# Half of the cross-attention transposes moved from TensorE to VectorE blocks and a trip through DRAM

## The chip, the cores and the metric

The kernel runs on one core of a Trainium2 chip. The metric is the time of one execution on the device in microseconds (us), the median of three runs. All times below come from the runs and from one profiled execution of the kernel before the change.

## What is computed

One decoder layer in float32 on `x` of shape (8, 256, 1024) with a context of the same shape: self-attention, cross-attention and a gated feed-forward network, each after a layer norm and each added to its input. Only the middle part is changed. Cut to it, the reference is

```python
def _L0_xattn_ref(Q, K, Wq_d, W_qk, Wkv_d, Wv_u):       # Q = layernorm(x), K = context
    C_q = Q @ Wq_d                                       # 1024 -> 128
    C_kv = K @ Wkv_d                                     # 1024 -> 64
    CqWqk = (C_q @ W_qk).reshape(b, n, H, LKV)           # 16 heads of 64
    scores = jnp.einsum('bnhl,bkl->bhnk', CqWqk, C_kv) / jnp.sqrt(...)
    attn = jax.nn.softmax(scores, axis=-1)
    V_up = (C_kv @ Wv_u).reshape(b, nkv, H, HD)
    out = jnp.einsum('bhnk,bkhd->bnhd', attn, V_up)
```

For each of the 8 batches and 16 heads there is a 256x256 matrix of probabilities. It is computed with the queries on the partitions, and its product with the values needs it the other way round, with the keys on the partitions. So every such matrix is turned. How it is turned is what the change is about.

## The kernel before, in words

**Stages.** The program runs self-attention for the 8 batches (64 steps of four heads), then cross-attention for the 8 batches (32 steps of four heads), then the feed-forward network. The loop at L1657-L1668 makes the steps. A batch of cross-attention has four steps, called c0 to c3 here.

**One cross step** is `step()` at L733, for the heads `j` = 0 to 3 of `cur`; `prev` is the step before, `due` the one before that. In the order in which each engine gets its instructions:

- `scores` (L669): TensorE multiplies the queries with the latent keys, 8 matmuls into four PSUM banks `pss0` to `pss3`, one per head. Each bank has one buffer, so a head's scores wait until the exponentials of that head in the step before have read it.
- `due.early()` (L707): VectorE copies the weighted product `po` of the step before last to `ol`.
- Per head, VectorE takes the maximum of each row (L743), and `turned(prev.p[j])` (L575) turns the previous step's probabilities: TensorE makes four 128x128 transposes into PSUM (L579) and ScalarE copies the result to the tile `pT` (L583).
- `due.late()` (L711): four matmuls with the value weights (L716), VectorE scales with 1/sum (L724), GpSimd adds to the residual rows `x1t` (L731).
- The exponentials: 8 ScalarE instructions, two per head (L762), each with a row sum. They are mixed with the *parts* of the queue: `step` keeps an account in which a part has a planned cost in us and an exponential 0.49, and issues exponentials ahead of a part as long as they are behind it.
- `prev.weighted(pTs)` (L693, called at L798) at the end of the step: 8 matmuls (L699) of the turned probabilities with the latent values, into `po`.

**Parts** are pieces of work for the next batch, written out by hand in `cross_plan` (L1501): in c0 two of the four `cqk` products (L941, L944) and the context's turning (L185); in c1 `ckv` (L855); in c2 `cq` (L925, copied by VectorE at L930); in c3 the small transposes L877, the first two `cqk` products, and `lnx` `first` (L904). In the first three batches an output projection of self-attention (`o_parts`) lies in some steps too, and three steps of the last batch hold a product of 16 large matmuls for the feed-forward network (L1123).

**`lnx` `first`** serves the batch after next. `send` normalises the rows (`normed_half`, L155, four 128x512 VectorE instructions at L157) and SyncE stores them to DRAM `n2` (L894). `take` reads them back in another order (`quarters_load`, L165: 32 partitions per DMA, four DMAs per tile, 1 KB runs, L168), so that 32x32 block transposes on VectorE (`turn32`, L181) make a full transpose of them. The same trick serves the context.

**Queues.** Each engine takes its instructions in program order (`tc.manual_schedule`, L1593). All loads, and all stores but those of GpSimd, are issued by SyncE in that order too, and a DMA that has to wait holds up the ones behind it. The feed-forward weights are loaded in the middle of cross-attention: `ffn_load_a` (L966) in c0 of batch 3, `ffn_load_b` (L977) in c0 of batch 4. `Head.norm` (L1073) normalises rows for the feed-forward network on GpSimd in c1 and c2 of batch 5 and in c3 of batch 6, each with a store by SyncE (L1080).

Of the kernel before, what the change touches and what calls it, by code (L numbers as in the profile page):

```python
# [18 lines left out]
P = 128  # L19
# [16 lines left out]
def decoder_layer(  # L36
# [117 lines left out]

    def normed_half(x_, mv, rs, h, tag="xn"):  # L155
        xn = wk_.tile([P, 512], F32, tag=tag, name="xn", bufs=2)
        nc.vector.tensor_scalar(  # L157
            xn, x_[:, h * 512 : (h + 1) * 512], mv, rs, ALU.subtract, ALU.mult
        )
        return xn  # L160
# [413 lines left out]

    def turned(p):  # L575
        ps = bank([P, TB, S], "ps_pt")
        for k in range(TB):
            for t in range(TB):
                nc.tensor.transpose(  # L579
                    ps[:, k, t * P : (t + 1) * P], p[:, t, k * P : (k + 1) * P], ident  # L580
                )
        pT = wk_.tile([P, TB, S], F32, tag="pT", name="pT", bufs=4)
        nc.scalar.copy(pT, ps)  # L583
        return pT

    class Self:


        def __init__(self, st, c):
            self.st, self.c = st, c  # L590

            self.by = st.by[c]
# [70 lines left out]
    class Cross:  # L663


        def __init__(self, st, c):
            self.st, self.c = st, c

# [24 lines left out]
        def weighted(self, pTs):  # L693

            self.po = pso.tile([P, 2, S], F32, tag="pso", name="po")
            for i in range(2):
                for k in range(TB):
                    for j in range(2):
                        nc.tensor.matmul(  # L699
                            self.po[XD * j : XD * (j + 1), i, :],  # L700
                            self.st.ckvT[:, k, :],
                            pTs[2 * i + j][:, k, :],
                            start=(k == 0),
                            stop=(k == TB - 1),
                        )

        def early(self):  # L707
            self.ol = wk_.tile([P, 2, S], F32, tag=("oh0a", "oh0b")[self.c % 2], name="ol")
            nc.vector.tensor_copy(self.ol, self.po)

# [22 lines left out]
    def step(cur, prev, parts, extra=None):  # L733
# [3 lines left out]
        cur.sm = small.tile([P, TB, 4], F32, tag="sm", name="sm")  # L737
        due = prev.prev if prev is not None else None
        if due is not None:
            due.early()  # L740
        pTs = []
        for j in range(4):
            nc.vector.tensor_reduce(nm[:, j, :], s[j], AX.X, ALU.max, negate=True)  # L743
            if prev is not None:
                pTs.append(turned(prev.p[j]))
        for p in queue[: min(parts, 2)]:
# [12 lines left out]
        def exp(j, t):  # L759
            if t == 0:  # L760
# [3 lines left out]
                bias=nm[:, j, t : t + 1], accum_out=cur.sm[:, t, j : j + 1],  # L764
            )

        exps = [(j, t) for j in range(4) for t in range(TB)]
# [29 lines left out]
        if prev is not None:  # L797
            prev.weighted(pTs)  # L798
            prev.prev = None
# [117 lines left out]
    def cq_part(st):  # L917
        box = {}

        def main(half):  # L920
# [258 lines left out]
    def unit(db, k, following, mid=None, jobs=((),) * 4, also=((),) * 3, sums_=(), last=False):  # L1179
# [39 lines left out]
        act(q7, c21)  # L1219
        ac2 = wide("pT", "ac2", 4)  # L1220
        stt(ac2, c12, bu, q7, ALU.add, ALU.add)  # L1221
# [279 lines left out]
    def cross_plan(b):  # L1501
# [91 lines left out]
    with tc.manual_schedule(  # L1593
# [257 lines left out]
```

## Time and profile before

| | |
|---|---|
| median of the 3 runs | 1460.16 us (1460.09 to 1461.78) |
| time of the profiled execution | 1462.0 us |
| its span, first to last instruction | 1460.2 us |
| granted TensorE clock, mean | 0.993 |
| busy share of the span: TensorE, VectorE, ScalarE, GpSimd | 97%, 74%, 58%, 42% |
| cross-attention, first to last scores | 629.1 to 949.1 us |
| one batch of it (799.97 to 837.54) | 37.57 us: steps of 9.25, 8.86, 10.22 and 9.24 |

The profile shows one execution. A group line names the source line, the engine, the operation, what is written and read, the count, the busy time and the mean duration in ns; behind the bar stands the idle time of the engine before these instructions and what ended it. In the trace, PE stands for TensorE's matmuls, PEld for its weight loads, DVE for VectorE, ACT for ScalarE, POOL for GpSimd and SP for SyncE. A float32 matmul other than a transpose is recorded as two instructions. Busy records overlap where matmuls are pipelined, so the duration of a group on the chain of waits tells its cost better than the mean duration of one.

### The profile page before, as it was taken

The page shows a single profiled execution, that of the slowest core. Times are in us where ns is not written, and L with a number is a line of the kernel's source. Part 1 is how long each engine was busy: PE and PEld are TensorE (multiplying, and loading weights), DVE is VectorE, ACT ScalarE, POOL GpSimd, SP SyncE. Part 2 cuts the span into 40 slices and gives each one's busy share as a digit, 9 for nine tenths or more (in the row PEclk, how much of TensorE's full clock was granted, in tenths as well). Part 3 has the DMA queues.
Part 4 walks back from the last instruction along what each step waited for, and adds up shares of the span by engine and source line. Part 5 has one row for each costly group of instructions (what it writes and reads, how often), then busy time and mean ns, then how long its engine had stood idle before and what let it go on. Part 6 is the DMA issues. An engine that isn't in the chain of part 4 may idle for free.

```text
span 1460.2 us, 25787 instructions
## 1 busy us (share of the span) xinstructions
PE 1422.7 (97%) x8946; PEld 954.7 (65%) x8946; DVE 1073.5 (74%) x2042; ACT 849.6 (58%) x2553; POOL 610.5 (42%) x769
## 2 busy tenths in 40 slices
PE   6899999999999999989999999999999999999998
PEld 6778888888888888667787777654444444444444
DVE  6888898989898989866777778447747645555664
ACT  4777898989898988856556666543313322223320
POOL 2544444444444443402232262435525424555740
PEclk9999999999999999989999999999999999999999
DMA  9620010101010124344448676723222000213003
GB/s 213 135 59 16 30 59 30 59 30 59 31 62 27 45 63 163 105 103 130 134 128 271 199 249 175 230 89 131 84 61 72 29 0 34 82 58 129 1 0 116
DMA packets 102961, 134.75 MB, mean 92 GB/s; under 512 B 44538, under 2 KB 75440, under 8 KB 102704
## 3 DMA queue, kind: packets, MB, share of 16 engines
q1 hardware_dynamic: 98224, 116.33, 27.2%
q0 software_dynamic: 4608, 16.78, 3.0%
q8 instruction: 72, 1.18, 0.3%
q14 instruction: 57, 0.47, 0.1%
HBM read 90.60 MB, written 41.94 MB: 91 GB/s over the span
## 4 chain that ended last, share of the span: by engine, by line
PE 54%; ACT 2%; DVE 2%; DMA 1%; issue 1%; SPq 0%; POOL 0%; ACTq 0%; DVEq 0%
PE c L1189 17%; PE z L1283 9%; PE ps_pt L579 4%; PE ps_o L1399 4%; PE s L676 4%; PE ps_p L1123 4%; PE po L699 3%; PE ps_o L716 2%; PE ps_q L925 2%; PE ps_qk L941 2%; ACT p L762 2%; PE ps_k L855 1%; PE ps_o L547 1%; PE ps_h L1252 0%; DMA n<-xn 0%
## 5 line engine op out<-in xcount | busy, mean ns | idle before, releaser
L762 ACT ACTIVATE p<-s,nm 128x256 f32<-128x256 f32 x768 | 358.4, 518 | 3.3 <-DVE nm L743 3.3
L583 ACT COPY pT<-ps_pt 128x512 f32<-128x512 f32 x384 | 197.7, 600 | 146.1 <-PE ps_pt L579 146.1
L743 DVE TENSOR_REDUCE nm<-s 128x2 f32<-128x512 f32 x384 | 237.5, 679 | 5.0 <-PE s L676 3.7
L579 PE MATMUL ps_pt<-ident,p 128*128 128x128 f32 x1536 | 198.9, 282 | 5.8 <-DVE p L623 2.5
L579 PEld LDWEIGHTS ps_pt<-ident,p 128*128 128x128 f32 x1536 | 167.4, 143 | 46.2 <-issue 24.2
L762 ACT ACTIVATION_READ_ACCUMULATOR p<-s,nm 128x1 f32 x768 | 191.8, 250 | 0.0
L1240 POOL TENSOR_TENSOR ac<-ac,sg 128x512 f32<-128x512 f32 x41 | 52.2, 1273 | 207.5 <-ACT sg L1239 207.5
L731 POOL TENSOR_TENSOR x1t<-x1t,y 128x256 f32<-128x256 f32 x64 | 46.3, 743 | 200.5 <-DVE y L724 200.5
L407 POOL TENSOR_SCALAR tmp<-y 128x512 f32<-128x512 f32 x78 | 60.1, 770 | 167.4 <-DVE y L556 91.3
L1189 PE MATMUL c<-t,s_v 128*128 128x512 f32 x252 | 122.2, 594 | 1.1 <-ACT q L1213 0.8
L454 PE MATMUL ps_q<-xh,qT_w 128*128 128x256 f32 x496 | 122.4, 288 | 0.0
L454 PE MATMUL ps_q<-xl,qT_w 128*128 128x256 f32 x496 | 119.6, 282 | 0.0
L1199 ACT COPY a<-c 128x512 f32<-128x512 f32 x42 | 24.6, 585 | 153.6 <-PE c L1189 153.6
L547 PE MATMUL ps_o<-oT_w,oh 128*128 128x512 f32 x256 | 106.4, 416 | 0.0
L547 PE MATMUL ps_o<-oT_w,ol 128*128 128x512 f32 x256 | 101.7, 397 | 0.0
L454 PEld LDWEIGHTS ps_q<-xh,qT_w 128*128 128x128 f32 x496 | 93.5, 188 | 1.6
L454 PEld LDWEIGHTS ps_q<-xl,qT_w 128*128 128x128 f32 x496 | 93.7, 189 | 0.0
L623 DVE TENSOR_SCALAR p<-p,sm 128x256 f32<-128x256 f32 x256 | 86.7, 396 | 8.4 <-PE ps_q L454 0.5
L1189 PEld LDWEIGHTS c<-t,s_v 128*128 128x128 f32 x252 | 47.4, 190 | 62.6 <-issue 50.3
L630 ACT ACTIVATE p<-p,sm 128x256 f32<-128x256 f32 x172 | 75.8, 513 | 18.9 <-DVE sm L613 18.3
L1221 DVE SCALAR_TENSOR_TENSOR ac<-c,b_col,q 128x512 f32<-128x512 f32 x42 | 31.5, 751 | 65.9 <-ACT q L1219 65.9
L600 PE MATMUL s<-kT,qT 32*128 32x256 f32 x1024 | 76.4, 403 | 3.7 <-DVE qT L412 2.4
(194 smaller groups left out, 3081.5 us busy)
## 6 DMA issues: line engine op xcount, KB each, us to landing
xs<-in_x_dram SPq DMA_DIRECT2D x32, 512.0 KB
x<-xs POOLq DMA_DIRECT2D x16, 512.0 KB, 3.1
x1t<-x SPq DMA_DIRECT2D x16, 512.0 KB
c<-in_ctx_dram SPq DMA_DIRECT2D x64, 128.0 KB
n<-xn SPq DMA_DIRECT2D x32, 256.0 KB
xp<-n SPq DMA_DIRECT2D x64, 128.0 KB
x<-x1t POOLq DMA_DIRECT2D x16, 512.0 KB, 5.6
x2n<-x SPq DMA_DIRECT2D x16, 512.0 KB
```

What stands on the lines that cost most here:

```text
L407: nc.gpsimd.tensor_scalar(tmp, y, 0.0, -1e6, ALU.min, ALU.max)
L454: nc.tensor.matmul(ps[:, i, :], w(i, e), x_[:, e, :], start=(e == 0 and x_ is st.xh), stop=(e == EC - 1 and x_ is st.xl),)
L547: nc.tensor.matmul(ps, o_[c // 4][:, c % 4, t * P : (t + 1) * P], oT_w[:, c, h * 512 : (h + 1) * 512], start=(c == 0 and o_ is st.oh), sto ...
L579: nc.tensor.transpose(ps[:, k, t * P : (t + 1) * P], p[:, t, k * P : (k + 1) * P], ident)
L583: nc.scalar.copy(pT, ps)
L600: nc.tensor.matmul(s[j][:, t, :], st.qT[p0 : p0 + 32, c, t * P : (t + 1) * P], st.kT[p0 : p0 + 32, c // 4, :], start=True, stop=True,)
L623: nc.vector.tensor_scalar_mul(p, p, self.sm[:, t, j : j + 1])
L630: nc.scalar.activation(p, p, AF.Copy, scale=self.sm[:, t, j : j + 1])
L743: nc.vector.tensor_reduce(nm[:, j, :], s[j], AX.X, ALU.max, negate=True)
L762: nc.scalar.activation(cur.p[j][:, t, :], s[j][:, t, :], AF.Exp, bias=nm[:, j, t : t + 1], accum_out=cur.sm[:, t, j : j + 1],)
L1189: nc.tensor.matmul(ps, w, x_, start=start, stop=stop, skip_group_check=True)
L1283: nc.tensor.matmul(db.X[key], w, x_, start=start, stop=stop or key == "1")
```

## The change

In each cross step, heads 2 and 3 are turned as before. Heads 0 and 1 go another way. As soon as their exponentials are done in their own step, VectorE turns them in 32x32 blocks into a tile `pB`, SyncE stores `pB` to DRAM (512 KB), and four DMAs (128 KB each, 1 KB runs, 32 partitions each) read it back with the quarters exchanged. The result `pD` holds the keys on the partitions, with the queries in runs of 32, and the weighted product reads it through a strided view. Since this takes time, the weighted product of a cross step is issued one step later: after the scores of the step after next, ahead of the transposes, with heads 2 and 3 first.

Other edits make room for it. The copy of `po` to `ol` goes from VectorE to ScalarE. The copy of `cq` goes from VectorE to ScalarE, and so does every other copy of `cqk` for the batches 1 to 7. The normalisation in `lnx` goes from VectorE to GpSimd. Tiles change places: `pT` has two buffers of two heads instead of four of one, `ol` uses the `v` buffers, `cq` a buffer of its own.

```diff
-    def normed_half(x_, mv, rs, h, tag="xn"):
+    def normed_half(x_, mv, rs, h, tag="xn", eng=None):
         xn = wk_.tile([P, 512], F32, tag=tag, name="xn", bufs=2)
-        nc.vector.tensor_scalar(
+        (eng or nc.vector).tensor_scalar(
...
+    both = [None]
+
+    def turned(p, j):
...
+        if j % 2 == 0:
+            both[0] = wk_.tile([P, 2, TB, S], F32, tag="pT", name="pT", bufs=2)
+        pT = both[0][:, j % 2]
         nc.scalar.copy(pT, ps)
         return pT
 
+    moved = [
+        dram.tile([P, 4, 2, P], F32, name=f"moved{i}") for i in range(B * XH // 4)
+    ]
+    crossed = [0]
+
+    def turned_blocks(cur):
+        n = crossed[0]
+        crossed[0] += 1
+        pB = wk_.tile([P, 4, 2, 4, 32], F32, tag="oh0b", name="pB")
+        for j in range(2):
+            src = cur.p[j].rearrange("p t (k c e) -> p c (t k) e", k=TB, c=4)
+            nc.vector.transpose(pB[:, :, j], src)
+        shape = [P, 4, 2, TB, TB, 32]
+        if n % 2:
+            pD = wk_.tile(shape, F32, tag="oh0a", name="pD")
+        else:
+            pD = wk_.tile(shape, F32, tag="pT", name="pD", bufs=2)
+        nc.sync.dma_start(moved[n], pB.rearrange("p c j m q -> p c j (m q)"))
+        for c in range(4):
+            nc.sync.dma_start(
+                pD[32 * c : 32 * c + 32].rearrange("p a j t k q -> p a (j t k q)"),
+                moved[n].rearrange("(a r) c j m -> r c a (j m)", a=4)[:, c],
+            )
+        for j in range(2):
+            cur.blocks[j] = pD[:, :, j]
+
+    def keys_of(pT, k):
+        if len(pT.shape) == 3:
+            return pT[:, k, :]
+        return pT[:, :, :, k, :].rearrange("p a t q -> p t a q")
+
+    def turned_of(prev, j):
+        return prev.blocks[j] if j in prev.blocks else turned(prev.p[j], j)
...
         def weighted(self, pTs):
             self.po = pso.tile([P, 2, S], F32, tag="pso", name="po")
-            for i in range(2):
+            for i in (1, 0):
...
-                            pTs[2 * i + j][:, k, :],
+                            keys_of(pTs[2 * i + j], k),
...
         def early(self):
-            self.ol = wk_.tile([P, 2, S], F32, tag=("oh0a", "oh0b")[self.c % 2], name="ol")
-            nc.vector.tensor_copy(self.ol, self.po)
+            self.ol = wk_.tile([P, 2, S], F32, tag="v", name="ol", bufs=2)
+            nc.scalar.copy(self.ol, self.po)
...
         due = prev.prev if prev is not None else None
+        if isinstance(due, Cross):
+            due.weighted(due.pTs)
         if due is not None:
             due.early()
...
-                pTs.append(turned(prev.p[j]))
+                pTs.append(turned_of(prev, j))
...
+            if (j, t) == (1, TB - 1) and not divided:
+                turned_blocks(cur)
...
         if prev is not None:
-            prev.weighted(pTs)
+            if isinstance(prev, Self):
+                prev.weighted(pTs)
+            prev.pTs = pTs
             prev.prev = None
...
-                    ("xn", "z")[t] if st.b > 1 else "xn",
+                    ("xn", "z")[t] if st.b > 1 else "xn", nc.gpsimd,
...
-                st.cq = wk_.tile([P, S], F32, tag="v", name="cq", bufs=2)
-                nc.vector.tensor_scalar_mul(st.cq, ps, 1.0 / 8.0)
+                st.cq = wk_.tile([P, W], F32, tag="cq", name="cq")[:, 0:S]
+                nc.scalar.activation(st.cq, ps, AF.Copy, scale=1.0 / 8.0)
...
-        k, q, t, u = ckv_part(x_), cq_part(x_), ckvT_part(x_), cqk_parts(x_, (dve, act))
+        k, q, t, u = ckv_part(x_), cq_part(x_), ckvT_part(x_), cqk_parts(x_, (act, act))
...
+        prev.prev.weighted(prev.prev.pTs)
         prev.prev.early()
-        pTs = [turned(p) for p in prev.p]
+        pTs = [turned_of(prev, j) for j in range(4)]
```

In the feed-forward network the tile `ac2`, which shares the `pT` buffers, is taken in pairs as well, and its last one uses the `cq` buffer.

More of the change, by code (lines that the diff above doesn't have):

```diff
@@ L572, in o_parts @@
         return [Part(2.0, lambda i=i: main(i)) for i in range(2)]
-    def turned(p):
+    both = [None]
+    def turned(p, j):
         ps = bank([P, TB, S], "ps_pt")
@@ L581, in turned @@
                 )
-        pT = wk_.tile([P, TB, S], F32, tag="pT", name="pT", bufs=4)
+        if j % 2 == 0:
+            both[0] = wk_.tile([P, 2, TB, S], F32, tag="pT", name="pT", bufs=2)
+        pT = both[0][:, j % 2]
         nc.scalar.copy(pT, ps)
         return pT
+    moved = [
[28 more added lines that the diff above has]
+        return prev.blocks[j] if j in prev.blocks else turned(prev.p[j], j)
     class Self:
         def __init__(self, st, c):
-            self.st, self.c = st, c
+            self.st, self.c, self.blocks = st, c, {}
             self.by = st.by[c]
@@ L666, in __init__ @@
         def __init__(self, st, c):
-            self.st, self.c = st, c
+            self.st, self.c, self.blocks = st, c, {}
         def scores(self):
@@ L1219, in unit @@
         act(q7, c21)
-        ac2 = wide("pT", "ac2", 4)
+        if k == FULL - 1:
+            ac2 = wide("cq", "ac2", 1)
+        else:
+            if k % 2 == 0:
+                both[0] = wk_.tile([P, 2, W], F32, tag="pT", name="ac2", bufs=2)
+            ac2 = both[0][:, k % 2]
         stt(ac2, c12, bu, q7, ALU.add, ALU.add)
```

## The prediction

> **What bounds the kernel now.** The chain of waits by engine comes first.
>
> ```profile
> PE 54%; ACT 2%; DVE 2%; DMA 1%; issue 1%; SPq 0%; POOL 0%; ACTq 0%; DVEq 0%
> ```
>
> TensorE carries almost all of it. (The chain could be followed back to 591 us only; the change acts behind that.) Next is one batch of cross-attention, first by busy times in a window, then as the chain in the order of time.
>
> ```profile
> 799.97:837.54 37.57, 37.52 (x293) 29.13 (x293) 27.45 (x54) 23.99 (x82) 7.70 (x12) 1.00 0.66 195
> ```
>
> ```profile
> 805.19 2.86 ACT p L762 x12
> ...
> 808.09 1.13 PE s L676 x6
> 809.22 1.98 PE ps_pt L579 x16
> 811.20 0.99 PE ps_o L716 x8
> 812.18 1.90 PE ps_k L855 x32
> ...
> 814.27 1.88 PE po L699 x16
> 816.14 1.93 PE s L676 x16
> ```
>
> TensorE is busy for 37.52 of 37.57 us, so a step lasts as long as its matmuls. But ScalarE shows in the chain at 805.19: its exponentials ended just late enough to hold the scores. It is idle a third of the time, yet it is the next limit.
>
> **TensorE's gain.** The 16 transposes of a step take 1.98 us, 0.124 each. Eight go: 0.99 us a step, 31.7 us in 32 steps, if nothing else becomes late. The moved product costs the same 1.88. Its strided operand has no row: from 0 (the same L699 row) to double for the four matmuls on it, +0.94 a step or +30 in all. I take 0, the row being the same instruction, and keep the other end. A gain is excluded, since columns and passes stay.
>
> **ScalarE's chain.** Let E be the end of a step's scores. Before, the transposes follow at E, the first copy to `pT` starts at E+0.7 (828.98 after 828.30), the exponentials at E+2.6 (830.89). After, the product (1.88) comes first, and ScalarE has the copy of `ol` at the head of its queue, behind it. It starts at E+2.1 (0.25 from a matmul's end to a copy, as in the rows); it and two `pT` copies, 0.51 apart like the four in 2.05, end at E+3.65. The exponentials start 1.05 later than before. They come 0.45 apart; the last score bank is free 0.15 after the eighth; three more matmuls (0.72) end the next scores. Copies of parts stand between the exponentials, where the account of L775 puts them, and wait for their matmuls (`late` ends at E+3.84):
> - c1: 3.65 + 3.6 + 0.15 + 0.72 = 8.1 (before 8.86).
> - c2: six exponentials, then `cq` at 3.84 + 3.46 + 0.25 = 7.55, 0.35 long, two exponentials: 9.7 (before 10.22).
> - c3: one exponential, the first `cqk` copy at 5.4, two exponentials, the second copy to 7.3, five exponentials: 10.4 (before 9.24).
> - c0: a `cqk` copy at 5.05, two exponentials, another to 6.95, six exponentials: 10.5 (before 9.25).
>
> A batch takes 38.7 against 37.6: 0.99 less on TensorE, and 1.1 more by ScalarE. Over six batches that is +7; the seven steps with `o_parts` or feed-forward matmuls stay bound by TensorE and gain 0.5 to 1 each, -5. **Sum of the loop: about +3.**
>
> **VectorE** gets two transposes (0.67 each, L185) and loses the `ol` copy (0.64): +0.7 a step, 2.8 a batch. It loses two `cqk` copies, a `cq` copy and four normalisations: 1.4 + 0.4 + 1.9. It is less busy than before (27.45 of 37.57), so I cost it at nothing; its cover would be gone if a transpose waited for `pB`, whose store must have landed.
>
> **The trip through DRAM.** The blocks of step n are needed in step n+2, in the second half of the product. Their DMAs stand in SyncE's queue behind whatever the step issued before. In that queue a wait holds up all the rest:
>
> ```profile
> SPq L894 <- DVE xn L157: 65.8, 10, 17.9
> SPq L1080 <- POOL x2n L1077: 43.6, 8, 18.8
> ...
> SPq L168 <- DMA w_ffn<-in_L_ffn_V_dram: 7.9, 1, 7.9
> ```
>
> The normalisation moves to GpSimd. The same operation on twice the width stands there already:
>
> ```profile
> L1077 POOL TENSOR_SCALAR x2n<-x2n,mv,rs x8: 3767/3771/3793, 853.2 to 921.3; 128x1024 f32<-128x1024 f32 x8
> ```
>
> Half of 3771 is 1.89 us, so four take 7.5 where VectorE's L157 took 1.9. The lowest row for the width is L407 (immediate operands, 0.77), the highest 3.77; I take 1.89 as it is the same operation. In c3 the account issues three exponentials ahead of `lnx`, and head 1's second, which releases the blocks, behind it. So the four `n2` stores and eight `xp` loads go ahead of the blocks. From E of c3: GpSimd's residual adds end at 6.3, the normalisations at 13.9, the last store lands at 16.5 (2.0 for a store, in the chain), the loads are issued by 18.5, their data (1 MB at 229 GB/s, window 838 to 842) flow until 20.5. The blocks' store (512 KB at 348 GB/s, window 842.5 to 845.5, 1.5, and 1.3 of latency, what is left of a 256 KB store's 2.01) lands at 22.8, their loads (2.3 of data, 1.3, 0.4 of issue) at 26.6. Needed at 10.4 + 10.5 + 0.94 = 21.9. **TensorE waits 4.3 to 4.7 us**, and as the `ol` copy and all exponentials stand behind it on ScalarE, nothing catches up. Six batches: **+26**.
>
> **Feed-forward loads.** In batch 3 c0 they are issued behind those late blocks (the fourth load at 22.8 + 1.8 = 24.6, which is 14.2 from c0's own E, 10.4 later), and c0's own blocks come behind them: 1 MB at 229 and 3.26 MB at 421 GB/s (window 776 to 782) with 1.3 of latency give E+27.6, the small bias loads 2, store 2.8, loads 4.0: E+36.4. Needed at 10.5 + 12.7 (c1 with its wait) + 0.94 = 24.1: **+12**. Five smaller ones: 2 MB of loads in c0 of batches 4 and 5 (6 us each at 348 GB/s against about 3.5 of slack), stores behind L1077 in batches 5 and 6 (7.5 and 15 us), eight loads more in c3 of batch 5: about 2.6 each, **+13**.
>
> **The clock.** TensorE's waits bring a second cost. Three windows show it, with the granted clock third from the right:
>
> ```profile
> 593.72:597.13 3.41, 1.06 (x6) 0.69 (x7) 3.37 (x7) 2.74 (x7) 1.95 (x2) 1.00 0.70 242
> 597.13:600.55 3.42, 3.42 (x11) 2.79 (x10) 2.64 (x7) 3.38 (x13) 1.68 (x3) 0.50 1.05 279
> ...
> 631.27:634.68 3.41, 0.95 (x8) 0.72 (x7) 1.50 (x5) 0.32 (x1) 0.00 (x0) 1.00 0.50 186
> 634.68:638.09 3.41, 2.69 (x10) 1.69 (x10) 3.41 (x8) 3.18 (x9) 0.00 (x0) 0.50 0.92 281
> ```
>
> A window that TensorE filled by 1.06 or 0.95 of 3.41 us was followed by one at half the clock, in the second case by three. One such window costs up to 1.7 us of work. Eight waits of 3 us and more (six, batch 3, batch 7): **+14**.
>
> The Trainium skill, "TensorE: Matmul & The Clock Gate", Part 1, has the gate close after a whole idle window of about 3.4 us. These rows are stricter: a third of a window busy did not prevent it. By the rule, our waits of 4.3 would seldom hold a whole window, and these 14 us would be near 0; I go by the rows. The skill's "VectorE: DVE Perf Modes", section "The three transpose paths", speaks against the change: VectorE turns 32x32 blocks only, and a whole 128x128 transpose belongs to TensorE. Its figures (311 ns against 390 in bf16) would make it a fair exchange; the trace's, 0.67 for a head against 0.50 plus a copy, say so too. What the rule leaves out is the trip for the rest.
>
> **Start of the stage.** Between 592 and 597 and between 631 and 635 VectorE waited for `xn` buffers while normalising, and TensorE stood for 2.4 and 2.6 us. With GpSimd these go (-3 to -8, with the clock), but the first batch's rows arrive some 6 us later, and VectorE waits for them. I take 0.
>
> **Sum**: 3 + 26 + 12 + 13 + 14 = +68 on the profiled execution's 1462.0 (span 1460.2), **1530 us**. The median of the runs is 1.8 lower, far inside the range.
>
> **Rivals.**
> - *The blocks come in time* (0.20). GpSimd normalises in 0.77 like L407, which saves 4.5 a batch and thereby the 26, and the loads hide. What is left is the loop with its +3 and some of the 25 at the feed-forward loads: 1463 to 1485. For it: VectorE and SyncE have room. Against: the L1077 row.
> - *TensorE's gain comes through* (0.12), the case on the other side: 1462 - 32 = 1430. It decides if exponentials end before TensorE's 7.7 us of a step. ScalarE would have to lose 1.1 a batch, 0.3 a step, for a gain to appear at all, and 2.8 in c0 for the whole. Against: its copies wait for a product and for `cqk` in program order.
> - *The clock stays low* (0.10), as for 10.2 us from 634.68 on: 8 waits cost up to 5 each, and doubled strided reads would add as much: 1570 to 1610.
> - That the change does not do what it says can't be: 256 transposes leave TensorE by the diff.
>
> **The numbers.** Forecast 0.58, rivals 0.20, 0.12, 0.10. The range leaves out the gain (0.12) and the worst of the slow rival (0.08): 1462 to 1595. A measurement tells 0.2% (3 us) from no change: faster 0.12, same 0.05 (a quarter of the first rival), slower 0.83.
>
> **What would show it.** Right: L579 has 1280 transposes; TensorE's longest waits are at L699 for a DMA of `pD`, in c1 of each batch and most in c2 of batch 3; L157 on GpSimd is near 1.9 us; windows at clock 0.5 in the middle of the stage; ScalarE's chain in c3 and c0. Wrong: no DMA in TensorE's waits; L157 below 1 us; c0 below 9.3 us.

## The result, and the profile after

The changed kernel takes 1567.9 us (median of four runs, 1566.2 to 1571.1); on the same chip the kernel before takes 1461.0. The ratio is 1.073, with an interval of 1.071 to 1.075: **107 us slower**. The forecast was 1530, slower with a chance of 0.83. The profiled execution took 1568.5, with a span of 1566.4 and a mean granted clock of 0.959 (before 0.993). Its lines are numbered by the changed file: the scores stand at L715, the product at L738, the transposes at L581, the exponentials at L803, the blocks at L602 (VectorE), L608 (store) and L610 (loads).

The chain of waits by engine, on the page of the changed kernel:

```profile
PE 42%; DMA 6%; POOL 6%; SPq 3%; DVE 2%; issue 2%; ACT 2%; DVEq 0%; POOLq 0%; ACTq 0%
```

DMA has grown from 1% to 6% and POOL from 0 to 6%, and SyncE's queue stands there with 3%. One batch, from the end of c0's scores in batch 4 to the same point of batch 5, as a window (length, then busy time of TensorE, its weight loads, VectorE, ScalarE and GpSimd, granted clock, DMA share, GB/s):

```profile
843.81:897.33 53.52, 41.14 (x262) 29.01 (x263) 27.19 (x52) 23.89 (x81) 17.50 (x17) 0.88 0.73 219
```

The same batch took 37.57 us, with TensorE busy for 37.52 of it. Now TensorE is idle for 12.4 us of 53.5, and it is busy for longer although 32 transposes are gone, partly since the clock is 0.88. What it waits for stands in its groups (window 632 to 1095, the columns as before: busy, mean ns, then idle time and what ended it):

```profile
L715 PE MATMUL s<-ckv,cqk 64*128 64x256 f32 x512 | 95.2, 426 | 19.2 <-ACT p L803 18.4 <-DVE y L763 0.8
...
L738 PE MATMUL po<-pD,ckv 128*64 128x256 f32 x256 | 45.3, 487 | 54.8 <-DMA pD<-moved 54.2 <-issue 0.4
```

Two waits, then: 54 us for the moved blocks, in 11 pieces, and 18 us for the exponentials, in 40 pieces of at most 0.7 (before there were 0.4 us of them). The first can be followed in the timeline, from c3 of batch 0 (whose scores end at 668.19) to the product that needs its blocks (start, length, engine, line, what; in brackets the idle time ahead and what ended it; other rows are left out here and in the timelines below):

```profile
674.86 8.25 POOL L157 TENSOR_SCALAR xn<-x1t,mv,rs 128x512 f32<-128x512 f32 x4
676.68 0.71 DVE L602 STREAM_TRANSPOSE pB<-p 128x512 f32<-128x512 f32 x1 [0.68 <-ACT p L803]
676.97 6.48 SPq L939 DMA_DIRECT2D n<-xn  x4
683.54 3.72 SPq L168 DMA_DIRECT2D xp<-n  x8
687.37 0.63 SPq L608 DMA_DIRECT2D moved<-pB  x1
691.49 1.73 SPq L610 DMA_DIRECT2D pD<-moved  x4
695.95 1.97 PE L738 MATMUL po<-pD,ckv 128*64 128x256 f32 x8 [4.68 <-DMA pD<-moved]
697.96 0.58 ACT L748 COPY ol<-po 128x512 f32<-128x512 f32 x1 [8.89 <-PE po L738]
```

VectorE has the blocks ready at 677.4. Their store is issued 10 us later, because SyncE's queue first sends the four rows that GpSimd normalises in 2.06 us each, then reads them back with eight loads. The blocks are there at 695.9, 18.5 us after they were ready, and TensorE has waited 4.7. The eight matmuls then take 1.97 us where the same eight of a step before took 1.03 (680.50): the granted clock has been halved meanwhile, which is called the closing of the clock gate below. ScalarE's copy of `ol`, with all exponentials behind it, has stood for 8.9.

**Where the 106 us of the span went.** From the end of the first scores of cross-attention to the end of the last, the records of both traces give this account. "Clock" is half of TensorE's busy time at half clock, an estimate that takes work to last twice as long there (1.97 for 1.03 above); "work" is its busy time less that. The two windows, columns as before:

```profile
631.20:949.07 317.87, 312.90 (x2282) 236.95 (x2283) 225.55 (x424) 187.75 (x640) 102.66 (x111) 0.98 0.62 184
638.63:1046.97 408.34, 330.68 (x2028) 231.85 (x2029) 215.03 (x398) 185.04 (x629) 154.99 (x137) 0.87 0.72 213
```

| us | before | after | difference |
|---|---|---|---|
| length (631.20 to 949.07; 638.63 to 1046.97) | 317.9 | 408.3 | +90.4 |
| idle for moved blocks | 0 | 51.9 | +51.9 |
| clock: half of the busy time at half clock (8.7; 73.1) | 4.4 | 36.6 | +32.2 |
| idle ahead of scores, for exponentials | 0.4 | 19.2 | +18.8 |
| other idle | 4.6 | 6.5 | +1.9 |
| work | 308.6 | 294.2 | -14.4 |

Outside it, 7.4 us more pass before the first scores, and 8.3 more behind the last. The work fell by 14 and not by the 32 of the transposes, because a matmul that starts early and waits in the pipeline counts as busy: the records of the scores cover 85.4 us, with half clock taken out as above, for 68.8 before, about 17 us of waits for exponentials in that form. Both kinds together (36) eat the saving.

### The profile page after: what moved, and what is told of

Read it like the earlier page. It is cut to its first block, busy times and chain, and to the rows that moved or that the text cites. A ratio compares the mean times of both kernels' runs of the same rounds, so it can differ in the third digit from the quotient of the medians.

```text
span 1566.4 us, 25398 instructions
## 1 busy us (share of the span) xinstructions
PE 1445.0 (92%) x8690; PEld 952.0 (61%) x8690; DVE 1062.4 (68%) x2020; ACT 847.6 (54%) x2543; POOL 674.3 (43%) x801
## 3 DMA queue, kind: packets, MB, share of 16 engines
q1 hardware_dynamic: 121264, 149.89, 32.2%
## 4 chain that ended last, share of the span: by engine, by line
PE 42%; DMA 6%; POOL 6%; SPq 3%; DVE 2%; issue 2%; ACT 2%; DVEq 0%; POOLq 0%; ACTq 0%
PE c L1234 15%; PE z L1333 8%; PE ps_o L1449 4%; PE po L738 3%; PE ps_p L1168 3%; POOL xn L157 3%; DMA moved<-pB 2%; PE ps_pt L581 2%; PE s L715 2%; POOL x2n L1122 2%; DMA pD<-moved 2%; PE ps_q L970 1%; SPq L168 1%; PE ps_o L755 1%; ACT p L803 1%
## 5 line engine op out<-in xcount | busy, mean ns | idle before, releaser
L803 ACT ACTIVATE p<-s,nm 128x256 f32<-128x256 f32 x768 | 358.3, 514 | 8.2 <-DVE nm L784 8.2
L587 ACT COPY pT<-ps_pt 128x512 f32<-128x512 f32 x320 | 167.0, 598 | 53.4 <-PE ps_pt L581 52.4
L803 ACT ACTIVATION_READ_ACCUMULATOR p<-s,nm 128x1 f32 x768 | 189.2, 246 | 0.0
L581 PE MATMUL ps_pt<-ident,p 128*128 128x128 f32 x1280 | 176.5, 292 | 9.7 <-POOL p L655 5.7
L581 PEld LDWEIGHTS ps_pt<-ident,p 128*128 128x128 f32 x1280 | 147.5, 149 | 52.9 <-issue 34.5
L407 POOL TENSOR_SCALAR tmp<-y 128x512 f32<-128x512 f32 x78 | 58.4, 748 | 163.5 <-DVE y L556 88.1
L748 ACT COPY ol<-po 128x512 f32<-128x512 f32 x32 | 18.8, 586 | 185.1 <-PE po L738 185.1
L715 PE MATMUL s<-ckv,cqk 64*128 64x256 f32 x512 | 95.2, 426 | 19.2 <-ACT p L803 18.4
L738 PE MATMUL po<-pD,ckv 128*64 128x256 f32 x256 | 45.3, 487 | 54.8 <-DMA pD<-moved 54.2
L763 DVE TENSOR_TENSOR y<-ps_o,sm 128x512 f32<-128x512 f32 x32 | 22.1, 689 | 105.4 <-PE ps_o L755 53.3
```

Source lines behind the costliest of these rows:

```text
L581: nc.tensor.transpose(ps[:, k, t * P : (t + 1) * P], p[:, t, k * P : (k + 1) * P], ident)
L715: nc.tensor.matmul(s[2 * i + j][:, t, :], st.cqk[p0 : p0 + XD, 2 * c + i, t * P : (t + 1) * P], st.ckv[p0 : p0 + XD, :], start=True, stop= ...
L738: nc.tensor.matmul(self.po[XD * j : XD * (j + 1), i, :], self.st.ckvT[:, k, :], keys_of(pTs[2 * i + j], k), start=(k == 0), stop=(k == TB ...
L803: nc.scalar.activation(cur.p[j][:, t, :], s[j][:, t, :], AF.Exp, bias=nm[:, j, t : t + 1], accum_out=cur.sm[:, t, j : j + 1],)
```

## The experiments

The theory at the start: the blocks arrive late because their DMAs stand behind `lnx` in SyncE's queue, and these waits close the clock gate, that is, halve the granted clock. Rival A: ScalarE's longer chain, with the product a step later, is what costs. Rival B: the trip through DRAM is too long in any order. The same account as above for all runs, each against the kernel before on its own chip (1460.4 to 1461.5); the columns on the right are differences to before over the stage of cross-attention.

| run | median us | ratio (interval) | stage | for blocks | for exponentials | clock | other idle | work |
|---|---|---|---|---|---|---|---|---|
| after | 1567.9 | 1.073 (1.071-1.075) | +90.4 | 51.9 | 18.8 | 32.2 | 1.9 | -14.4 |
| e1_norm_dve | 1541.4 | 1.055 (1.050-1.061) | +68.5 | 42.3 | 19.5 | 14.7 | 4.9 | -12.9 |
| e2_blocks_first | 1529.4 | 1.047 (1.044-1.050) | +55.3 | 24.2 | 19.3 | 23.6 | 2.0 | -13.8 |
| e3_late_only | 1514.1 | 1.037 (1.033-1.041) | +43.0 | 0 | 18.9 | 9.2 | -2.5 | +17.2 |
| e4_warm | 1576.1 | 1.079 (1.072-1.087) | +95.4 | 43.4 | 19.3 | 23.8 | 2.2 | +6.7 |
| e5_old_place | 1533.8 | 1.050 (1.049-1.052) | +69.0 | 78.8 | 0.7 | 18.6 | 1.0 | -30.2 |
| e6_blocks_relieved | 1529.9 | 1.047 (1.046-1.049) | +59.0 | 35.3 | 13.8 | 14.5 | 10.0 | -14.7 |
| e7_late_relieved | 1493.7 | 1.023 (1.021-1.025) | +32.8 | 0 | 13.8 | 3.3 | 0.3 | +15.3 |
| e8_norm_alone | 1472.2 | 1.007 (1.006-1.009) | +1.6 | 0 | 0 | -1.8 | 3.8 | -0.5 |
| e9_old_place_pool | 1571.1 | 1.076 (1.074-1.078) | +106.6 | 103.4 | 0 | 34.6 | 2.8 | -34.3 |
| e10_late_pool | 1550.3 | 1.061 (1.059-1.063) | +91.0 | 48.9 | 18.5 | 30.4 | 5.6 | -12.4 |
| e11_some_steps | 1505.0 | 1.030 (1.029-1.032) | +40.2 | 50.5 | 0.7 | 7.9 | 0.3 | -19.2 |
| e12_some_steps_cqk | 1504.1 | 1.028 (1.026-1.030) | +41.3 | 52.8 | -0.3 | 12.1 | -0.6 | -22.7 |

The columns are those of one profiled execution. In e1, e3, e4, e9, e10 and e11 it lies 2 to 7 us from the median (e4: 1580.7 for 1576.1; e10: 1557.1 for 1550.3), and the columns fit the median only so far.

**e1_norm_dve**: the normalisation back on VectorE.

```diff
-                    ("xn", "z")[t] if st.b > 1 else "xn", nc.gpsimd,
+                    ("xn", "z")[t] if st.b > 1 else "xn",
```

> The changed kernel with one edit: the normalisation in lnx goes back from GpSimd to VectorE. Theory (blocks arrive late behind lnx in SyncE's queue, and each wait closes the clock gate): four instructions of 2.07 us become four of 0.54, the rows leave 6 us sooner, the waits of 4.7, 1.6, 6.0 and 4.9 us for pD in c1 of batches 1 to 4 go, the 9.3 of batch 6 shrinks, and so do half-clock windows behind them: about 1535 us (1525 to 1545). Rival A (the cost is ScalarE's longer chain with the product ahead of it): 1563 to 1573, no change. Rival B (the trip through DRAM is too long in any order): the waits stay, 1555 or more.

1541 is in the theory's range: 26 us less than the change. In the stage the waits for blocks fell by 10 and the clock's share by 17.5; 8 more are saved outside it.

**e2_blocks_first**: GpSimd still normalises, but the first four exponentials, and with them the blocks and their DMAs, are issued ahead of the parts that send and take rows.

```diff
-            while exps and sc < pe:
+            while exps and (sc < pe or (not divided and queue[0].yields and len(exps) > 4)):
...
-        return [Part(0.0, first)] + [Part(0.0, lambda t=t: turn(t)) for t in range(TB)]
+        a = Part(0.0, first)
+        a.yields = True
+        return [a] + [Part(0.0, lambda t=t: turn(t)) for t in range(TB)]
...
+            p.yields = us == 0.0
```

> The changed kernel with one edit: ahead of lnx and of the feed-forward rows' parts (norm, take), step issues the first four exponentials, so that the blocks' DMAs stand before those parts in SyncE's queue; GpSimd still normalises. Theory: the same waits in c1 go, and with them those behind the feed-forward norms (9.3, 5.0, 4.4); what stays is batch 3 (10.8) and part of c2 of batch 4: about 1518 us (1505 to 1535), and a lower time than with the normalisation moved back alone. Rival A: 1563 to 1573. Rival B: 1555 or more.

1529, lower than e1, as the theory said. The waits for blocks halved, to 24, and 15.2 of that is one wait behind the feed-forward loads. So SyncE's order is a cause. But the kernel stays 69 us slower than before, with most blocks in time.

**e3_late_only**: no blocks; all four heads are turned by TensorE; the product still comes a step later, and the copies and the normalisation stay where the change put them.

```diff
-            if (j, t) == (1, TB - 1) and not divided:
-                turned_blocks(cur)
```

> The changed kernel without the blocks: TensorE turns all four heads, no trip through DRAM, but the product is still issued a step later with the copy of ol on ScalarE. Theory: no wait for a DMA; the exponentials start another 1.0 us later in each step (four copies of pT ahead of them, E+4.65), so the steps c0 to c3 take 11.5, 9.1, 10.7 and 11.4 us, 42.7 a batch against 37.6 before: 1460 + 30 for the loop and 0 to 20 for the clock, 1500 us (1485 to 1515). Rival A (ScalarE's chain is nearly all of the 107 us): 1550 or more. Rival B (the trip is all of it): 1455 to 1465.

1514 is within the theory's range and fits neither rival's number. What it shows is more than that: half of the 107 us, 54, is there **without any block**. The theory of late blocks explains the other half only. In this run 256 transposes are back on TensorE, and scores still wait 18.9 us more for exponentials, with another 17 hidden in "work", which should have stayed the same. The normalisation and the copies have a part in the 54 (see e7).

**e4_warm**: 24 transposes of the identity into an unread bank between the halves of the product of each c3. They add to the computation and change nothing in the output.

```diff
             for i in (1, 0):
+                if i == 0 and self.c == 3:
+                    spare_ = bank([P, TB, S], "ps_spare")
+                    for m in range(24):
+                        nc.tensor.transpose(spare_[:, m % 2, 0:P], ident, ident)
```

> The changed kernel with 24 transposes of the identity (nothing reads them) between the two halves of the product of each c3, that is, in the place where TensorE waits 4.7 us. They add work and take away no wait. Theory (half clock behind the waits costs some 25 to 40 us in all): TensorE stays busy, half-clock time falls by 20 to 40 of the 113 us, and the time falls although work is added: 1550 to 1562 us. Rival (the clock costs nothing to speak of, since ScalarE or the DMA sets the pace anyway): 1566 to 1575 us, with less time at half clock or not.

1576, 8 us more: the theory's 1550 to 1562 fell, and the rival's 1566 to 1575 is just missed. The account shows why the run doesn't decide on the clock by itself. Time at half clock fell from 104 to 72 us and the clock's share by 8.4, the waits for blocks by 8.5; the transposes take 22 us of TensorE in the stage. Keeping the clock up this way costs more than it brings.

**e5_old_place**: the product goes back to the end of the next step; with it the edits of e1 and e2. Two heads still go through DRAM.

```diff
-        if isinstance(due, Cross):
-            due.weighted(due.pTs)
...
-            if isinstance(prev, Self):
-                prev.weighted(pTs)
-            prev.pTs = pTs
+            prev.weighted(pTs)
```

> The blocks alone: the product goes back to the end of the next step (where the kernel before has it), the normalisation back to VectorE, and the first four exponentials and the blocks' DMAs go ahead of the parts that issue lnx; two heads of four are still turned through DRAM. Theory (the later place of the product costs by itself, +54 in the run with no blocks, and the blocks' trip fits into one step when nothing stands ahead of it in SyncE's queue): the steps are bound by TensorE again and lose 0.99 us of transposes each (31.7 in all), the blocks land 12 to 14 us behind the scores where the product needs them at about 13, and only the batch with the feed-forward loads waits long (some 15): 1435 to 1470. Rival (the trip is too long in any order; a product one step earlier leaves it one step less): waits of 5 us or more in most steps, 1500 or more.

1534: my theory fell, and the rival's 1500 or more came, though waits of 5 us and more stand in six steps only and not in most. The saving is there at last (work -30.2, no waits for exponentials), but the blocks come too late in c1 of batches 1 to 6. Timeline around it (c0's scores end at 679.02):

```profile
683.99 1.50 DVE L603 STREAM_TRANSPOSE pB<-p 128x512 f32<-128x512 f32 x2
684.84 4.83 SPq L168 DMA_DIRECT2D xp<-n  x8
...
689.79 0.35 SPq L609 DMA_DIRECT2D moved<-pB  x1
...
693.61 2.13 SPq L611 DMA_DIRECT2D pD<-moved  x4
...
700.19 1.98 PE L739 MATMUL po<-pD,ckv 128*64 128x256 f32 x8 [7.76 <-DMA pD<-moved]
```

The blocks are ready at 685.5, and usable 14.7 us later: 4.3 in SyncE's queue behind eight loads of `xp`, 3.8 for the store, 6.6 for the loads. The blocks of c3 just before, with nothing ahead of them in the queue and only the stores of `lnx` behind, were ready at 676.76 and used at 683.99: 7.2 us.

**e6_blocks_relieved**: e2 with the normalisation, the copies of `ol` and `cq` and one of the two `cqk` copies back on VectorE.

```diff
-            nc.scalar.copy(self.ol, self.po)
+            nc.vector.tensor_copy(self.ol, self.po)
...
-                nc.scalar.activation(st.cq, ps, AF.Copy, scale=1.0 / 8.0)
+                nc.vector.tensor_scalar_mul(st.cq, ps, 1.0 / 8.0)
...
-        k, q, t, u = ckv_part(x_), cq_part(x_), ckvT_part(x_), cqk_parts(x_, (act, act))
+        k, q, t, u = ckv_part(x_), cq_part(x_), ckvT_part(x_), cqk_parts(x_, (dve, act))
```

> The run with the blocks ahead (1529), and besides it the normalisation, the copies of ol and cq and one of the two cqk copies back on VectorE; the product stays a step later. Theory that the longer chain on ScalarE is the second price beside the late blocks: 3.9 us a batch leave ScalarE (four copies of 0.59, two of 0.59, one of 0.38), c0 and c3 fall from 10.6-11.5 to about 9.5: 1500 to 1518. Rival (only the late blocks and the clock count; VectorE, busier by as much, delays the blocks instead): 1525 to 1540.

1530 against e2's 1529: no gain from the four moves together. Scores wait 5.5 us less, but the waits for blocks grow (35.3 for 24.2), all in c2 of batches 3 to 6. These blocks, counted from the end of c0's scores, are used after 35.9, 26.5, 25.0 and 28.5 us, and after 36.1, 25.3, 25.2 and 28.2 in e2: the trip sets the time, and what the steps save turns into longer waits. Of the 10.0 of other idle time, 1.0 is for `ol` itself, now behind VectorE's queue.

**e7_late_relieved**: no blocks, every copy and the normalisation on its old engine. Of the change only the place of the product is left, with the order of its halves and the places of the tiles. Its edits are those of e3, e1 and e6.

> No blocks, all four heads on TensorE, every copy and the normalisation on the engine of the kernel before: of the change only the place of the weighted product is left, a step later, ahead of the transposes. It ran at 1514 with the copies on ScalarE. If the copies on ScalarE were the price (3.9 us a batch, 31 in all): 1460 to 1470 plus what the place costs. The place by hand: the four copies of pT and so the exponentials start 1.9 later behind the product, so c0, c1 and c3 take 9.0 to 10 us where they took 8.5 to 9.25, 1.5 to 2.5 a batch: 1472 to 1490 is what I expect. If the copies do not matter: 1500 or more. If the place is free: 1455 to 1466.

1494, just above the 1472 to 1490 I gave: **the place alone costs 33 us**. The step c0 of batch 1 in the chain of waits:

```profile
678.06 1.88 PE po L738 x16
679.94 1.97 PE ps_pt L581 x16
681.91 0.99 PE ps_o L755 x8
682.90 1.74 PE ps_qk L984 x8
...
685.15 2.86 ACT p L803 x12
688.01 0.04 issue
688.05 1.13 PE s L715 x6
```

A c0 of the kernel before (9.24 us, from 799.98) has the same chain but for the product at its head:

```profile
799.98 1.98 PE ps_pt L579 x16
801.95 0.99 PE ps_o L716 x8
802.94 1.74 PE ps_qk L941 x8
...
805.19 2.86 ACT p L762 x12
808.05 0.04 issue
808.09 1.13 PE s L676 x6
```

In e7 the chain goes through TensorE's product, transposes, `late` and the `cqk` part before it reaches the exponentials, and then waits for them. From 684.6 to 688.0 TensorE can only follow the exponentials head by head, because the product, which used to fill this gap at the end of the step, has been done at its start. The step takes 11.12 for 9.24, longer by the product's 1.88; so does c3, c1 takes 9.45 for 8.52, and c2, which TensorE's matmuls fill, is as long as before. e3 less e7 is 20 us. If the prices add, the normalisation (e8) is 11 of it, and some 9 are left for the copies on ScalarE.

**e8_norm_alone**: the kernel before with one edit, the normalisation of `lnx` on GpSimd.

```diff
-        nc.vector.tensor_scalar(
+        (eng or nc.vector).tensor_scalar(
...
-                    ("xn", "z")[t] if st.b > 1 else "xn",
+                    ("xn", "z")[t] if st.b > 1 else "xn", nc.gpsimd,
```

> The kernel before with one edit: the normalisation of lnx on GpSimd. With the blocks it cost 27 us (1568 against 1541). Theory (it costs only because the blocks' DMAs stand behind its stores in SyncE's queue): without blocks the next batch's xp is some 6 us later and has a step and more of slack, so 1456 to 1468. Rival (the slow normalisation is late for the next batch itself): 1475 or more.

1472, between the theory's 1456 to 1468 and the rival's 1475: it costs 11 us by itself. 29 of 31 steps are the same to 0.35 us. The 11 come from two places. The first scores end at 640.63 for 631.20, and the first step gets 6.2 of that back. And c3 of batch 3 takes 17.2 for 9.7: everything in SyncE's queue is later, so the feed-forward loads and, behind them, `ckv`, for which TensorE waits 5.65. Together with e1 (26 saved in the changed kernel) this leaves some 15 us that GpSimd's normalisation costs only where blocks stand behind it, if the prices add.

**e9_old_place_pool** and **e10_late_pool**: the blocks' store and loads issued from GpSimd, in e5, and in e2 with the normalisation on VectorE.

```diff
-        nc.sync.dma_start(moved[n], pB.rearrange("p c j m q -> p c j (m q)"))
+        nc.gpsimd.dma_start(moved[n], pB.rearrange("p c j m q -> p c j (m q)"))
...
-            nc.sync.dma_start(
+            nc.gpsimd.dma_start(
```

> As the run with the product back in its old place (1534), and besides it the blocks' store and their four loads issued from GpSimd instead of SyncE. In that run the store of c0's blocks stood 4.3 us behind eight xp loads in SyncE's queue (transposes done at 685.5, store issued at 689.8), and TensorE waited 78 us for pD in all, 7 to 10 in c1 of most batches and 21 behind the feed-forward loads. Theory (SyncE's order is what makes the blocks late): the waits of c1 fall by 4 to 6 each and the long one by 10 or more; 1460 to 1495. Rival (the trip itself, store, landing and loads, with the other traffic on the same DMA engines, is what is too long): the store goes out earlier but lands as late; 1515 or more.

> The product a step later as in the changed kernel, the blocks ahead of the other parts, the normalisation on VectorE, and the blocks' store and loads issued from GpSimd. Theory (SyncE's order): nearly no wait for pD is left but behind the feed-forward loads; the steps are then the floors of the run with the norm on VectorE (10.6, 10.6, 8.5, 12.9 where the run of the product's place alone has 11.1, 11.1, 9.45, 13.95), 24 us less than its 1494 at best and a few of waits more: 1472 to 1500. Rival (the trip itself): 1515 or more.

1571 and 1550: the theory that only SyncE's order is wrong fell twice. (The counterpart of e10 with SyncE's queue was not run; the nearest, e2 and e6, took 1529 and 1530.) In e9, the blocks of c3 of batch 0, ready at 683.04 (these scores end at 674.18, the next at 686.70):

```profile
683.34 0.70 POOL L609 DMA_DIRECT2D moved<-pB  x1 [1.29 <-DVE pB L603]
685.89 4.90 SPq L168 DMA_DIRECT2D xp<-n  x8
688.08 2.21 POOL L611 DMA_DIRECT2D pD<-moved  x4 [4.04 <-PE ps_pt L582]
690.89 7.41 SPq L168 DMA_DIRECT2D c<-in_ctx_dram  x8
697.39 1.97 PE L739 MATMUL po<-pD,ckv 128*64 128x256 f32 x8 [6.04 <-DMA pD<-moved]
```

The store goes out at once. It has landed at 687.5, and the four loads, issued from 688.1 on, land at 692.9, 694.6, 695.5 and 697.2, beside 1 MB of `xp` and 1 MB of context that SyncE's queue now sends at the same time. The trip takes 14.4 us, where the same blocks took 7.2 in e5. Rival B is right as far as this: beside the other traffic the trip is longer than a step, whichever queue issues it. It does not explain all of e9: before three of its waits (8.7, 11.4 and 10.8 of the 103) the store stood 5 to 14 us in GpSimd's own queue. The Trainium skill, "DMA: Bandwidth & Descriptors", section "Issuing engines are not separate DMA queues", says that DMAs of all issuing engines run on the same 16 engines and interleave, and that a second issuing engine saves only the time to issue. This case agrees: for the blocks of c0 in batch 1, 4.0 us of queue were saved (4.3 in e5, 0.3 here), and the time from the store's issue to the last landing rose from 10.3 to 12.3.

**e11_some_steps** and **e12_some_steps_cqk**: e5, with blocks in c1, c2 and c3 of batches 0 to 2 and in c1 and c3 of the later ones; in e12 also one `cqk` copy back on VectorE.

```diff
-            if (j, t) == (1, TB - 1) and not divided:
+            if (j, t) == (1, TB - 1) and not divided and cur.c in ((1, 2, 3), (1, 3))[cur.st.b > 2]:
...
-        if n % 2:
+        if cur.c % 2:
```

> The run with the product in its old place and the blocks' DMAs on SyncE, but blocks only where that run hardly waited for them: c1, c2 and c3 of batches 0 to 2, c1 and c3 of the later ones; all other heads are turned by TensorE. That run's steps with blocks in time took 8.73 for 9.24 (c0, c3) and 12.9 or 9.2 for 13.95 or 10.2 (c2): 2.1 us less in each of three batches and 1.5 in each of five, 14 in all. Theory (the blocks pay where a step's slack holds the trip, and nothing else of the change is needed): 1444 to 1458. Rival (a trip disturbs whatever is beside it, by TensorE's clock, SyncE's queue or VectorE, so the waits move to the next transfer): 1465 or more.

> The same, with the first of the two cqk copies of a step back on VectorE, as before the change. In c0 and c3 ScalarE stood idle for that copy's matmuls (680.8 to 681.8) ahead of the exponentials; without it the exponentials end 1 to 1.5 us earlier and these steps can fall to TensorE's 8.25: 0.5 less in 14 steps, 7 in all. Theory: 1437 to 1452. Rival (VectorE's copy comes ahead of the transposes and makes the blocks late): 1460 or more.

1505 and 1504, and the rival's "1465 or more" came. Yet the account splits. Up to c1 of batch 3, that is with all nine moved products of batches 0 to 2, e11 is ahead of the kernel before: these scores end at 772.11 for 779.88, 5.7 us gained in the loop and 2.0 ahead of it. Then four waits of 18.4, 8.1, 8.8 and 6.9 us follow, each for the blocks of c1. The first of them, SyncE's queue alone:

```profile
773.23 1.65 SPq L1040 DMA_DIRECT2D b_row<-in_L_ffn_b_dram  x2
782.13 5.63 SPq L168 DMA_DIRECT2D c<-in_ctx_dram  x8
787.85 1.11 SPq L911 DMA_DIRECT2D ckv<-ckv  x2
789.07 0.52 SPq L609 DMA_DIRECT2D moved<-pB  x1
792.30 1.73 SPq L611 DMA_DIRECT2D pD<-moved  x4
```

Between 774.9 and 782.1 nothing is issued while the feed-forward weights flow; the context and `ckv` then go ahead of the store. In e12, c0 and c3 fall to 8.20 where nothing is late, as expected, and the same stretch gains 4.0 in the loop. By these two executions a version with blocks in batches 0 to 2 alone should be some 4 to 6 us faster than the kernel before, an estimate; it was not run, and so no version here beats it.

## Why the prediction was right, and where it was off

The forecast's mechanism came, and 1568 lies in the range. Step by step:

- **What bounds the kernel** and **ScalarE as the next limit**: right. Steps without a wait for blocks or half clock took 8.5 in c1 (forecast 8.1; e2, batch 3), 9.8 in c2 (9.7; e2, batch 4), 10.61 in c3 (10.4) and 10.60 in c0 (10.5): 39.5 a batch for 38.7. The +3 for the loop is +4.4 in the account (18.8 - 14.4). e7 shows what lies behind it, which the forecast did not say: without blocks the later place costs 33, so the blocks' whole gain of some 30 was spent before a single one was late.
- **VectorE at nothing**: the sum needs no term for it, but the condition named there occurred. Its transposes waited 51.4 us in 11 pieces for the one buffer `pB`, whose store had not landed. What a second buffer would save was not tried.
- **The trip in c3**: right almost to the step. Forecast from E of c3: normalisations done at 13.9, data at 26.6, needed at 21.9. Measured in batch 0 (E = 668.19): 14.9, 27.7 and 23.1. GpSimd's 1.89 was 2.07. Waits of 4.3 to 4.7 in six batches, 26 in all, were forecast; in c1 of batches 1 to 6 they were 4.7, 1.6, 6.0, 4.9, 0.4 and 9.3, 27 in all. The sum is partly luck: the 9.3 stands behind feed-forward rows too, and in batch 5 half clock had made TensorE late itself.
- **Feed-forward loads**: 12 forecast, 10.8 measured. The five smaller ones, 13 forecast: 4.2, 4.4 and 0.5 in c2 and c3 of batches 4 and 5, 5.0 in c1 of batch 7 behind the feed-forward rows that GpSimd normalises, and 2.9 behind the stage, 17 in all; the 9.3 in batch 6 holds another. All waits for blocks: 51 forecast, 54.2 measured.
- **The strided operand at nothing**: right. The median matmul on `pD` takes as long as that on `pT` (380 ns), where clock and waits are the same.
- **The clock: the mis-sized term.** Forecast were eight half-clock windows of 1.7 each, 14 in all. Measured are 14 stretches of 104 us in the stage, 30 windows and not eight, with TensorE busy for 73 of it: 32 us more than before. Two things were wrong. A stretch lasted 2.2 windows on average and not one, as the row of 634.68 had already shown with three. And half of the stretches do not follow a wait for a DMA at all. Here are six windows of 3.4 us around 693 and 728, columns as before:

```profile
690.10:693.50 3.40, 1.17 (x9) 0.49 (x8) 1.94 (x5) 0.00 (x0) 0.00 (x0) 1.00 0.41 136
693.50:696.95 3.45, 1.00 (x6) 0.71 (x8) 1.80 (x4) 0.00 (x0) 0.00 (x0) 0.50 0.75 240
696.95:700.30 3.35, 3.35 (x18) 2.59 (x15) 0.00 (x0) 1.61 (x3) 0.00 (x0) 0.50 0.52 155
724.20:727.60 3.40, 2.30 (x10) 1.26 (x10) 1.42 (x2) 3.40 (x15) 3.40 (x3) 1.00 0.01 2
727.60:731.00 3.40, 3.35 (x14) 1.95 (x16) 2.68 (x5) 0.00 (x0) 3.40 (x3) 0.50 0.24 88
731.00:734.40 3.40, 3.40 (x18) 2.07 (x15) 0.00 (x0) 0.58 (x1) 3.18 (x2) 0.50 0.40 148
```

  The first three are the wait for blocks that the forecast meant. In the next three no DMA is late: TensorE is recorded busy for 2.30 of 3.40 us, with ten matmuls that wait for exponentials (ScalarE is busy all the time), and the clock is halved all the same. Seven of the 15 stretches up to 1070 us follow such a window, 0.58 to 0.73 busy. Not every such window counts: of the windows of 3.41 us at full clock in the stage, one after the other from a change of the clock on, all 7 that were less than 0.50 busy were followed by half clock, 7 of the 13 between 0.50 and 0.75, and none of the 69 above. That the exponentials' waits and not the DMA set these was not tried by itself; e3 (five stretches, 27 us) and e7 (three, 17 us), where no block is moved, have such stretches too: all five in e3 after windows of 0.58 to 0.73, two in e7 after windows of 0.70 and 0.79. So the forecast's condition, a wait of 3 us or more for a DMA, was too narrow.
- **Start of the stage, taken as 0**: half right. The stage began 7.4 us later, and the first step gave 6.1 back. e8 names the cause: with the normalisation on GpSimd and nothing else, the same scores are 9.4 late and 6.2 come back; with it on VectorE (e1) they are 0.8 early. In the account the 6.1 lie inside the stage, so the start is 1.3 net.
- **Not in the sum**: 8.3 us behind the stage, where the last product waits 2.9 for its blocks and runs at half clock until 1069.

So of the 38 us between 68 forecast and 106, the clock is 18, the two ends of the stage are 16 (6 of it given back inside the stage), and the rest (other idle, loop and blocks) is 4.

The rivals: "the blocks come in time" would have had no waits at `pD`; "TensorE's gain comes through" fell with ScalarE's chain, as said there. "The clock stays low" had a part of the truth: its price for the clock, up to 40, is near the measured 32, without doubled reads.

**The cause, as the runs leave it.** The change asks for two things that exclude each other in the two places tried for the product. With the product in its old place the blocks save 30 us of TensorE's work, but have less than a step for a trip that takes 7.2 us with little beside it and 14 to 18 beside `xp`, context and feed-forward loads (e5, e9, the changed kernel). With the product a step later most blocks can be in time (e2), but that place itself takes 33 us (e7), since nothing is left to fill TensorE's time while ScalarE computes exponentials. GpSimd's normalisation adds 11 to 26 (e8, e1), and half clock charges nearly all of the long gaps and some of the short ones again. A third place was not run: at the end of the step after next the product would fill the gap again and the blocks would have longer. Open too is how much of the clock's 32 us belongs to the exponentials' gaps and how much to the blocks'; e4 moved both at once.

## What to carry to other kernels

Before work is taken off a full engine, look at what its removal and its new place leave to do while the next engine computes: a moved instruction that filled a gap is worth up to its own length there, whatever it costs elsewhere (here 33 us, 1.88 in each c0 and c3, for a product whose duration had not changed). A trip through DRAM is to be sized beside the traffic that runs with it and from the position in the queue, not alone: 7 us became 14 to 18. And gaps are to be counted twice, once for the time and once for the clock, and that can hold for short gaps that add up to a third of a window (7 of 13 such windows here).

## What the runs showed of the hardware

- **The clock gate** closed behind 7 of 13 windows that were 0.50 to 0.75 busy by the records (see above), and of the 14 stretches at half clock in the changed kernel's stage seven lasted 6.8 us, three 10.2 and one 17.1; only three were 3.4 or less. The Trainium skill, "TensorE: Matmul & The Clock Gate", Part 1, names a whole idle window as the condition, and its section "A second HAM failure mode: psum-queue depth-cycling" has a kernel whose frequent short idle times between groups of matmuls made the clock swing. The rows here agree with the second; a whole idle window was not needed.
- **GpSimd** took 2.07 us for (x - mean) x rstd on 128x512 with both operands from a column of memory, against 0.54 on VectorE in the kernel before, and 0.76 for the 128x512 operation with immediate operands on GpSimd (L407 of the changed kernel; all medians).
- **DMAs issued by GpSimd** (`pD`, e9) were sent 0.54 us apart, those by SyncE (e5) 0.47. From the issue of a 512 KB store to that of its first load, which waits for its landing, 5.3 us passed with GpSimd and 4.3 with SyncE (medians of 32), so the blocks were no earlier for GpSimd's queue.
